# One transformer block on one core: another beginning (order of loads, constants and first stages, and extra identity products on TensorE)

## The chip, the cores and the metric

The kernel runs on one core of a Trainium2 chip. A core has five engines that each run their own list of instructions in order and meet through semaphores: TensorE (PE; its weight loads are shown as PEld), VectorE (DVE), ScalarE (ACT), GpSimd (POOL) and SyncE (SP), which in this kernel only issues DMAs. The metric is the device time of one execution in microseconds. The kernel before took 459.29 us (median of 5 executions, 456.32 to 459.85).

## The reference, cut to what matters

Eight batches of 256 tokens of width 256 pass through an adaptive layer norm, an attention with a window of 64, a second adaptive layer norm and a mixture of 16 experts. Everything that this change touches lies before the first attention scores.

```python
mod = (_silu(L0_c) @ L0_wmod).reshape(8, 6, 1, -1)          # scales, shifts and gates of each batch
sa, ca, ga, sb, cb, gb = (mod[:, i] for i in range(6))       # ga, gb: sign kept, magnitude at least 0.25
h = _layernorm(x) * (1 + ca) + sa
q, k, v = h @ Wq.T, h @ Wk.T, h @ Wv.T                       # rotary embedding on q and k,
q = _layernorm_unit(rope(q)) * 256; k = _layernorm_unit(rope(k)); v = _layernorm_unit(v)
probs = softmax(30 * tanh((q @ k.T / sqrt(32) + mask) / 30))
x = x + ga * ((probs @ v) @ Wo.T)
h = _layernorm(x) * (1 + cb) + sb
x = x + gb * (experts(h, top 4 of 16) + shared(h))
```

## The kernel before, in words

All data is float32. A batch b is a tile `x_b` of 128 partitions by 2 by 256. The first part of the kernel (up to about 185 us) does attention, second norm and routing for the eight batches, software-pipelined: while the scores of batch b are computed, the qkv projection of batch b+2 and the norm of batch b+3 run. Then the tokens, scattered to rows in DRAM by expert, are fetched tile by tile and go through the experts; at the end sums are read back and the result is written.

In the first part the order on PE, DVE and ACT is written out by hand: `when(stage, batch)` emits the instructions of a stage, and each of these three engines runs what was emitted in exactly that order. POOL and SP are ordered by a scheduler; on POOL the helper `in_turn` (L387) forces the named operations into the order in which they were emitted.

The stages of the beginning, with the lines at which they show in the profile:

- Loads (SP, L106 to L144), in this order: c, a third of wmod (`load_mod(0)`, L116), x of batch 0 (L124), wqkv (L126), rope, x of batches 1 and 2, and so on. SP later issues the zero fills `rows_d<-none` and `sums<-none` (L285), the gates `gates_d<-g` (L455), the shared experts' weights, and the row of gates of each batch (`gate<-gates_d`, L474).
- Constants on POOL (L147 to L280): the identity `ident`, `nhalf`, masks, one-hot patterns, counters, and `none`, from which the zero fills are written.
- `condition_stage`: transposes c on PE (L412) and computes silu on DVE and ACT into `scT` (L414 to L420).
- `columns_stage(0)`: 16 products of wmod with `scT` on PE (L429), copied by DVE into `modT` (L433, L434).
- `fold_stage`: two DVE operations that take the mean out of the v columns of wqkv (L461, L462); they wait for wqkv.
- `stats_stage(b)`: the mean and variance of x_b on DVE (L468, L469), then `power` on POOL: an addition (L397) and a power of -0.5 (L398) give `rs`.
- `norm_stage(b)`: `nmr` on DVE (L482), then the normed x on ACT (L487, one instruction for each half).
- `turn_norm_stage(b)`: four PE transposes `pt_a` (L365), then ACT applies `modT` and gives `hT` (L374, two instructions).
- `qkv_stage(b, t)`: two PE matmuls, shown as four passes of 128x384 (L515), then rotary embedding on DVE (L526, L531, L537) and a copy of v on ACT (L536).
- `centre_stage(b)`: two DVE operations over q and k (L545, L546), then squares on ACT (L551, L552).
- `unit_stage(b)`: DVE sums the squares into `rstd` (L560), POOL raises 24 columns of it to the power -0.5 (L397, L398).
- `heads_stage(b)`: DVE multiplies q and k by `rstd` (`qn` L571, `kn` L580), POOL does v (L586); `turn_stage(b)` transposes them on PE (`pt_q`, `pt_k`).
- `rows_stage`: gates on PE (L442), five DVE operations (L449 to L454), the DMA to `gates_d`.

A PSUM tile of the helper `misc` comes from a pool of two buffers; `pt_a`, `pq`, the products of wmod and those of c share them.

Of the kernel before, what the change touches and what calls it, by code (L numbers as in the profile page):

```python
# [9 lines left out]
F32 = mybir.dt.float32  # L10
# [4 lines left out]
ALU = mybir.AluOpType  # L15
# [17 lines left out]
E, INTER, NSH = 16, 176, 2  # L33
TOPK, G, TOPK_G = 4, 4, 2
# [4 lines left out]
CAP = NTOK  # L39
# [5 lines left out]
Q0 = P + SW  # L45
LIVE = P + Q0
HIDDEN = -16.0

ROW = HID + 2 * E
# [9 lines left out]
NOWHERE = float(1 << 20)  # L59
# [8 lines left out]
MAXL = MAXT - MAXA  # L68
# [10 lines left out]
def kernel(  # L79
# [18 lines left out]
    nc = tc.nc  # L98

    const = ctx.enter_context(tc.tile_pool(name="const", bufs=1))  # L100
# [10 lines left out]
    def load_mod(n):  # L111
        nc.sync.dma_start(
            out=wmod_sb[:, :, n * 512 : (n + 1) * 512], in_=wmod_v[:, :, n * 512 : (n + 1) * 512]
        )

    load_mod(0)  # L116
    xs = []
    for b in range(B):
        xs.append(keep.tile([P, NT, HID], F32, tag="x", name=f"x_{b}"))
# [1 line left out]
    def load_x(b):  # L121
        nc.sync.dma_start(out=xs[b], in_=x_in[b].rearrange("(t p) d -> p t d", p=P))

    load_x(0)  # L124
    wqkv_sb = const.tile([P, NK, NH * D], F32)
    nc.sync.dma_start(out=wqkv_sb, in_=wqkvT.rearrange("(k p) n -> p k n", p=P))  # L126
    rope_sb = const.tile([P, NT, 2, D], F32)
# [10 lines left out]
        out=bias_sb,  # L138
        in_=expert_bias.rearrange("(o e) -> o e", o=1).to_broadcast([P, E]),
# [16 lines left out]
    nc.gpsimd.memset(maskb, 0.0)  # L156
    for lo, n in ((0, P), (P, Q0)):
        nc.gpsimd.affine_select(
            out=maskb[:, lo : lo + n], in_=maskb[:, lo : lo + n], compare_op=ALU.is_ge, fill=HIDDEN,
            base=0, pattern=[[1, n]], channel_multiplier=-1,  # L160
        )
        nc.gpsimd.affine_select(
            out=maskb[:, lo : lo + n], in_=maskb[:, lo : lo + n], compare_op=ALU.is_ge, fill=HIDDEN,
            base=SW - 1, pattern=[[-1, n]], channel_multiplier=1,
        )

    pmask = const.tile([P, P], F32)
    nc.gpsimd.memset(pmask, -1.0)
# [1 line left out]


    probs = [const.tile([P, REP, P + S], F32, name=f"probs_{i}") for i in range(KV)]
    for pr in probs:
        nc.gpsimd.tensor_copy(
            pr[:, :, LIVE : P + S], pmask[:, 0 : S - Q0].unsqueeze(1).to_broadcast([P, REP, S - Q0])
        )

    lowG = const.tile([P, G, G], F32)
    nc.gpsimd.memset(lowG, 1.0)
    nc.gpsimd.affine_select(  # L180
        out=lowG, in_=lowG, compare_op=ALU.is_gt, fill=0.0,
        base=0, pattern=[[1, G], [-1, G]], channel_multiplier=0,
    )

    before = const.tile([P, P], F32)
    nc.gpsimd.memset(before, 1.0)
    nc.gpsimd.affine_select(
        out=before, in_=before, compare_op=ALU.is_gt, fill=0.0,
        base=0, pattern=[[1, P]], channel_multiplier=-1,
    )  # L190
    ones = const.tile([P, P], F32)
    nc.gpsimd.memset(ones, 1.0)


    SUMS = KV * NT
    onehot = const.tile([P, SUMS, D], F32)
    nc.gpsimd.memset(onehot, 0.0)
    spread = const.tile([P, SUMS, P], F32)
    nc.gpsimd.memset(spread, 0.0)
    for m in range(SUMS):  # L200
        nc.gpsimd.memset(
            onehot[:, m, :].rearrange("p (a i) -> p a i", i=SUMS)[:, :, m : m + 1], 1.0
        )
        nc.gpsimd.affine_select(
            out=spread[:, m, :].rearrange("p (j d) -> p j d", d=D),
            in_=spread[:, m, :].rearrange("p (j d) -> p j d", d=D),
            compare_op=ALU.not_equal, fill=1.0, base=-m, pattern=[[-D, REP], [0, D]],
            channel_multiplier=1,
        )

    st = const.tile([P, B, NT, 6], F32)
    mv = const.tile([P, B, NT, 2], F32)
    rs = const.tile([P, B, NT], F32)
# [4 lines left out]
    def apart(ins, group):  # L218
# [10 lines left out]
    nc.vector.memset(acc, 0.0)  # L229

    first = const.tile([P, E], F32)
    nc.gpsimd.iota(
        first, pattern=[[CAP, E]], base=1, channel_multiplier=0,
        allow_small_or_imprecise_dtypes=True,
    )

    tno = const.tile([E, MAXL], F32)
    nc.gpsimd.iota(
        tno, pattern=[[1, MAXL]], base=0, channel_multiplier=0,
        allow_small_or_imprecise_dtypes=True,  # L240
    )
    eno = const.tile([P, E], F32)
    nc.gpsimd.iota(
        eno, pattern=[[1, E]], base=0, channel_multiplier=0,
        allow_small_or_imprecise_dtypes=True,
    )
    start = const.tile([E, 1], F32)
    nc.gpsimd.iota(
        start, pattern=[[0, 1]], base=-E * CAP, channel_multiplier=CAP,
        allow_small_or_imprecise_dtypes=True,  # L250
    )
    upto = const.tile([E, E], F32)
    nc.gpsimd.memset(upto, 1.0)
    nc.gpsimd.affine_select(
        out=upto, in_=upto, compare_op=ALU.is_ge, fill=0.0,
        base=0, pattern=[[1, E]], channel_multiplier=-1,
    )


    rows_d = tc.dram_tile([E * CAP + P, ROW], F32, name="rows_d")  # L260
    none = const.tile([P, ROW], F32)
    nc.gpsimd.memset(none[:, 0 : HID + E], 0.0)
    nc.gpsimd.memset(none[:, HID + E : ROW], NOWHERE)

    sums = [tc.dram_tile([NTOK + P, HID], F32, name=f"sums_{i}") for i in range(2)]
    spare = const.tile([P, 1], F32)
    nc.gpsimd.iota(
        spare, pattern=[[0, 1]], base=NTOK, channel_multiplier=1,
        allow_small_or_imprecise_dtypes=True,
    )  # L270
    pno = const.tile([P, 1], F32)
    nc.gpsimd.iota(
        pno, pattern=[[0, 1]], base=0, channel_multiplier=1, allow_small_or_imprecise_dtypes=True,
    )

    tokens = const.tile([P, B, NT, ROW - HID - E], F32)
    nc.gpsimd.iota(
        tokens, pattern=[[S, B], [1, NT], [0, ROW - HID - E]], base=0, channel_multiplier=NT,
        allow_small_or_imprecise_dtypes=True,
    )  # L280
# [61 lines left out]
    with ExitStack() as actx:  # L342
# [8 lines left out]
        def misc(name):  # L351
            return small_ps[0].tile([P, 512], F32, tag="mm", name=name)
# [34 lines left out]
        def in_turn(kind, ins):  # L387

            ins = getattr(ins, "ins", ins)
            for other in last:  # L390
                if kind != "put" or other != "put":
                    tc.add_manual_dep(ins, last[other], BEHIND, reason="order of GpSimd")
            last[kind] = ins.name

        def power(out, in_, eps):

            in_turn("own", nc.gpsimd.tensor_scalar(out, in_, eps, None, ALU.add))  # L397
            in_turn("own", nc.gpsimd.tensor_tensor(out, out, nhalf[:, 0 : in_.shape[-1]], ALU.pow))  # L398
# [574 lines left out]
        when(norm_stage, 0)  # L973
        when(stats_stage, 1)
        when(columns_stage, 0)
        when(turn_norm_stage, 0)
        when(stats_stage, 3)
        when(norm_stage, 1)
        when(qkv_stage, 0, 1)
        when(qkv_stage, 0, 0)  # L980
        when(turn_norm_stage, 1)
        when(centre_stage, 0)
# [12 lines left out]
        for b in range(B):  # L995
# [64 lines left out]
            out=gbs, in_=gates_d[1:2].rearrange("a b d -> a (b d)").to_broadcast([P, B * HID])  # L1060
# [285 lines left out]
```

## Time and profile before

| what | us |
|---|---|
| five executions | 458.76, 459.85, 459.29, 459.45, 456.32 |
| the profiled execution | 458.84 |
| its span, from the first to the last instruction | 456.9 |
| PE, DVE, ACT, POOL busy | 404.8, 257.6, 193.3, 236.5 |
| first `nmr` of batch 0 on DVE | 10.40 |
| first `qn` of batch 0 on DVE | 29.01 |

The span is cut into a beginning, in which engines wait for loads and for each other, and a long middle in which PE is busy nine tenths of the time. In the profile's timeline a row has the start in us, the length in us, the engine, the line, the operation, the tiles (output first) and, in brackets, the idle time of the engine before it with what ended it. Rows that follow each other without a gap are merged. A matmul in float32 shows as two passes. The chain of waits has the start, the length and the engine with tile and line.

### The profile page before, as it was taken

Reading aid. Unit: us, or ns where it says so; the run is one execution under the profiler, and the core shown is the slowest. Engines: PE = TensorE matmul, PEld = TensorE weight load, DVE = VectorE, ACT = ScalarE, POOL = GpSimd, SP = SyncE. Lnnn points to the kernel's source line nnn. Section 1 sums busy time; section 2 is a strip of 40 time slices with the busy share of each in tenths; the row PEclk is TensorE's granted clock in tenths of the full one; section 3 lists DMA queues with packets and bytes.
Section 4 is the critical chain, followed back from the end, with each engine's and each line's share of the span. In section 5 each row is a group of like instructions: output and inputs, shape, how many; then the busy total and the mean of one; then the engine's idle time right before and its main releaser. Section 6 shows DMA issues by size and latency. Waiting matters only on the chain.

```text
span 456.9 us, 8848 instructions
## 1 busy us (share of the span) xinstructions
PE 404.8 (89%) x2790; PEld 287.4 (63%) x2790; DVE 257.6 (56%) x937; ACT 193.3 (42%) x445; POOL 236.5 (52%) x232
## 2 busy tenths in 40 slices
PE   3878999998888857978999999999999999999763
PEld 3446777667666655555677657576777777777332
DVE  5677888987874543265764335425444454434087
ACT  2437788676645614225434321213434444343100
POOL 8155652486867641113566527755565656665200
PEclk9989999999999877797999999999999999999897
DMA  8999973012221210403455525555667666666494
GB/s 266 369 355 316 317 191 104 14 66 82 84 70 40 105 66 8 151 13 113 111 131 132 141 65 86 83 75 96 114 109 118 106 121 112 110 110 100 58 362 167
DMA packets 52926, 59.79 MB, mean 131 GB/s; under 512 B 5272, under 2 KB 47888, under 8 KB 52752
## 3 DMA queue, kind: packets, MB, share of 16 engines
q1 hardware_dynamic: 39728, 40.59, 30.1%
q0 software_dynamic: 13152, 18.62, 22.9%
q8 instruction: 24, 0.39, 0.4%
q14 instruction: 22, 0.18, 0.1%
HBM read 31.51 MB, written 27.69 MB: 130 GB/s over the span
## 4 chain that ended last, share of the span: by engine, by line
PE 69%; DVE 10%; DMA 9%; ACT 5%; issue 3%; POOL 2%; another core or an unknown queue 1%; SPq 1%; DVEq 0%; ACTq 0%; POOLq 0%
PE u L1115 16%; PE py L1141 11%; PE us L1172 7%; DMA sums<-yr,to 7%; PE pq L515 4%; PE pv L648 3%; PE pw L700 3%; PE sm L657 3%; PE xt L1083 3%; PE pz L1188 3%; PE ph L1130 3%; PE sc L621 2%; PE pn L679 2%; PE pr L724 2%; PE sc L612 1%
## 5 line engine op out<-in xcount | busy, mean ns | idle before, releaser
L1155 POOL DMA_INDIRECT sums<-yr,to x70 | 109.2, 1560 | 60.6 <-DVE h L1123 19.4
L928 POOL DMA_INDIRECT rows_d<-pay,idx x64 | 63.2, 988 | 79.7 <-ACT xT L1085 18.7
L1115 PE MATMUL u<-w,xT 128*128 x288 | 98.5, 465 | 0.4 <-issue 0.3
L1141 PE MATMUL py<-w_sb,hT 88*128 x280 | 72.0, 379 | 0.0
L1115 PEld LDWEIGHTS u<-w,xT 128*128 128x128 f32 x288 | 49.6, 192 | 17.0 <-issue 1.3
L1085 ACT COPY xT<-xt 128x256 f32<-128x256 f32 x73 | 27.1, 372 | 73.4 <-PE xt L1083 65.4
L1123 DVE TENSOR_TENSOR h<-h,u 128x176 f32<-128x176 f32 x72 | 24.2, 336 | 50.2 <-ACT h L1122 47.2
L1141 PEld LDWEIGHTS py<-w_sb,hT 88*128 88x128 f32 x280 | 47.6, 190 | 3.8
L1172 PE MATMUL us<-h2T,sw_sb 128*128 128x512 f32 (+1 forms) x96 | 46.0, 630 | 2.6 <-PEq L1258 2.6
L1122 ACT ACTIVATE h<-u 128x176 f32<-128x176 f32 x72 | 22.8, 317 | 58.1 <-PE u L1115 52.4
L1148 DVE TENSOR_SCALAR yr<-py,w 128x256 f32<-128x256 f32 x70 | 33.6, 480 | 11.3 <-PE py L1141 9.1
L1172 PEld LDWEIGHTS us<-h2T,sw_sb 128*128 128x128 f32 (+1 forms) x96 | 18.4, 195 | 25.4 <-issue 25.1
L398 POOL TENSOR_TENSOR rstd<-rstd,nhalf 128x24 f32<-128x24 f32 x8 | 33.8, 4221 | 0.7
L1089 DVE SCALAR_TENSOR_TENSOR both<-eno,whose,xr 128x16 f32<-128x16 f32 x73 | 16.8, 231 | 25.6 <-DMA xr<-rows_d 23.9
L515 PE MATMUL pq<-wqkv_sb,hT 128*128 128x384 f32 x64 | 27.4, 559 | 3.4 <-ACT hT L374 2.0
L1130 PEld LDWEIGHTS ph<-ident,h 128*88 128x88 f32 x142 | 17.2, 122 | 21.0 <-issue 12.2
L1083 PE MATMUL xt<-ident,xr 128*128 128x128 f32 x146 | 28.3, 276 | 0.0
L1188 PE MATMUL pz<-sw_sb,hs 128*128 128x256 f32 (+1 forms) x96 | 24.1, 403 | 4.1 <-DVE hs L1179 3.8
L1130 PE MATMUL ph<-ident,h 128*88 128x128 f32 x142 | 27.2, 273 | 0.4 <-DVE h L1123 0.4
L630 ACT ACTIVATE probs<-sc 128x640 f32<-128x640 f32 x32 | 22.3, 695 | 11.3 <-PE pw L700 9.1
L1132 ACT COPY hT<-ph 88x256 f32<-88x256 f32 x71 | 26.1, 367 | 1.6 <-PE ph L1130 1.4
L1083 PEld LDWEIGHTS xt<-ident,xr 128*128 128x128 f32 x146 | 20.4, 144 | 9.2 <-issue 3.1
(223 smaller groups left out, 657.8 us busy)
## 6 DMA issues: line engine op xcount, KB each, us to landing
xr<-rows_d SPq DMA_DIRECT2D x75, 144.0 KB
w<-in_w_dram SPq DMA_DIRECT2D x16, 352.0 KB
sums<-none SPq DMA_DIRECT2D x2, 2176.0 KB
got<-sums SPq DMA_DIRECT2D x16, 256.0 KB
w_sb<-in_w_dram SPq DMA_DIRECT2D x8, 352.0 KB
rows_d<-none SPq DMA_DIRECT2D x1, 2304.0 KB
x<-in_x_dram SPq DMA_DIRECT2D x8, 256.0 KB
out_dram<-got SPq DMA_DIRECT2D x8, 256.0 KB
```

Of the source, the lines that this page charges most:

```text
L398: in_turn("own", nc.gpsimd.tensor_tensor(out, out, nhalf[:, 0 : in_.shape[-1]], ALU.pow))
L515: ins = nc.tensor.matmul(out=pq[:, 0 : NH * D], lhsT=hT[:, k, t * P : (t + 1) * P], rhs=wqkv_sb[:, k, :], start=(k == 0), stop=(k == NK - 1),)
L928: ins = nc.gpsimd.indirect_dma_start(out=rows_d[:, :], out_offset=bass.IndirectOffsetOnAxis(ap=idx[:, t, k : k + 1], axis=0), in_=pay[:, t ...
L1083: nc.tensor.transpose(pt[:, k, :], x[:, k * P : (k + 1) * P], ident)
L1085: nc.scalar.copy(xT, pt)
L1115: ins = nc.tensor.matmul(out=pu, lhsT=xT[:, k, :], rhs=w13[:, k, bass.ds(e, 1), :].rearrange("p o h -> p (o h)"), start=(k == 0), stop=(k ...
L1130: nc.tensor.transpose(ph[:, i, :], h[:, i * HALF : (i + 1) * HALF], ident)
L1141: nc.tensor.matmul(out=py, lhsT=h[:, i, :], rhs=w2_sb[:, i, bass.ds(e, 1), :].rearrange("p o d -> p (o d)"), start=(i == 0), stop=(i == 1),)
L1148: nc.vector.tensor_scalar(y, py, w, None, ALU.mult)
L1155: ins = nc.gpsimd.indirect_dma_start(out=sums[len(added) % 2][:, :], out_offset=bass.IndirectOffsetOnAxis(ap=to[:, 0:1], axis=0), in_=y, i ...
L1172: nc.tensor.matmul(out=pus[a][:n], lhsT=sw13_sb[:, k, a, c : c + n], rhs=h2T[:, k, b0 : b0 + nb, :], start=(k == 0), stop=(k == NK - 1),)
L1188: nc.tensor.matmul(out=pz[:, t, :], lhsT=hids[b, i][:n, t * P : (t + 1) * P], rhs=sw2_sb[:n, i, :], start=(i == 0), stop=(i == len(SHC) - 1),)
```

## The change

Four things are moved or added; no arithmetic of the result is changed.

1. Loads: x of batch 0 is issued ahead of the first third of wmod.
2. Constants: only `ident`, `nhalf` and `pmask` are made at once. All the others are put in a list `fills`, and `fill_stage(0)` and `fill_stage(1)` emit the first and the second half of it, each in turn with the powers on POOL.
3. `warm_stage(n)`: n products of the identity with itself (float32, 128x128x128) into a `misc` tile that nobody reads: three before the transposes of c, five after.
4. The order of the stages.

```diff
-    load_mod(0)
...
     load_x(0)
+    load_mod(0)
...
+    fills = []
+    def fill(name, *args, **kwargs):
+        fills.append((name, args, kwargs))
...
-    nc.gpsimd.tensor_copy(identb, ident)
...
+    fill("tensor_copy",identb, ident)
+    fill("memset",maskb, 0.0)
...
+        def fill_stage(i):
+            n = len(fills) // 2
+            for name, args, kwargs in (fills[:n], fills[n:])[i]:
+                in_turn("own", getattr(nc.gpsimd, name)(*args, **kwargs))
+
+        def warm_stage(n):
+            pw = misc(f"warm_{n}")
+            for _ in range(n):
+                nc.tensor.matmul(out=pw[:, 0:P], lhsT=ident, rhs=ident, start=True, stop=True)
...
+        warm_stage(3)
         when(condition_stage, 0)
+        when(stats_stage, 0)
+        warm_stage(5)
         when(fold_stage, 0)
-        when(stats_stage, 0)
-        when(stats_stage, 2)
         when(norm_stage, 0)
-        when(stats_stage, 1)
+        fill_stage(0)
         when(columns_stage, 0)
+        when(stats_stage, 1)
+        fill_stage(1)
         when(turn_norm_stage, 0)
-        when(stats_stage, 3)
-        when(norm_stage, 1)
-        when(qkv_stage, 0, 1)
         when(qkv_stage, 0, 0)
-        when(turn_norm_stage, 1)
+        when(qkv_stage, 0, 1)
         when(centre_stage, 0)
+        when(norm_stage, 1)
+        when(stats_stage, 2)
+        when(turn_norm_stage, 1)
         when(norm_stage, 2)
         when(qkv_stage, 1, 0)
         when(unit_stage, 0)
+        when(stats_stage, 3)
         when(rows_stage, 0)
         when(columns_stage, 1)
```

In the built program two more things are seen. The first `power` of batch 0 stands on POOL directly behind the identity; that of batch 1 stands in the middle of the fills, behind the fill of `spread`; those of batches 2 and 3 behind all fills. And on SP the order of the zero fills is another: before, rows_d, one of the two `sums`, then `gates_d<-g`, then the other `sums`; after, `sums`, rows_d, `sums`, then `gates_d<-g`. From the first scores on, PE, DVE and ACT run the same lists as before.

More of the change, by code (lines that the diff above doesn't have):

```diff
@@ L150 @@
     nc.gpsimd.memset(nhalf, -0.5)
+    fills = []
+    def fill(name, *args, **kwargs):
+        fills.append((name, args, kwargs))
     identb = const.tile([P, P], BF16)
-    nc.gpsimd.tensor_copy(identb, ident)
     maskb = const.tile([P, LIVE], BF16)
[L156 to L165, printed above, removed]
     pmask = const.tile([P, P], F32)
@@ L172 @@
     probs = [const.tile([P, REP, P + S], F32, name=f"probs_{i}") for i in range(KV)]
[L173 to L176, printed above, removed]
     lowG = const.tile([P, G, G], F32)
[L179 to L183, printed above, removed]
-    before = const.tile([P, P], F32)
[L186 to L190, printed above, removed]
+    before = const.tile([P, P], F32)
     ones = const.tile([P, P], F32)
-    nc.gpsimd.memset(ones, 1.0)
     SUMS = KV * NT
     onehot = const.tile([P, SUMS, D], F32)
-    nc.gpsimd.memset(onehot, 0.0)
     spread = const.tile([P, SUMS, P], F32)
[L199 to L209, printed above, removed]
     st = const.tile([P, B, NT, 6], F32)
@@ L231 @@
     first = const.tile([P, E], F32)
-    nc.gpsimd.iota(
+    tno = const.tile([E, MAXL], F32)
+    eno = const.tile([P, E], F32)
+    start = const.tile([E, 1], F32)
+    upto = const.tile([E, E], F32)
+    rows_d = tc.dram_tile([E * CAP + P, ROW], F32, name="rows_d")
+    none = const.tile([P, ROW], F32)
+    sums = [tc.dram_tile([NTOK + P, HID], F32, name=f"sums_{i}") for i in range(2)]
+    spare = const.tile([P, 1], F32)
+    pno = const.tile([P, 1], F32)
+    tokens = const.tile([P, B, NT, ROW - HID - E], F32)
+    fill("tensor_copy",identb, ident)
+    fill("memset",maskb, 0.0)
+    for lo, n in ((0, P), (P, Q0)):
+        fill("affine_select",
+            out=maskb[:, lo : lo + n], in_=maskb[:, lo : lo + n], compare_op=ALU.is_ge, fill=HIDDEN,
+            base=0, pattern=[[1, n]], channel_multiplier=-1,
+        )
+        fill("affine_select",
+            out=maskb[:, lo : lo + n], in_=maskb[:, lo : lo + n], compare_op=ALU.is_ge, fill=HIDDEN,
+            base=SW - 1, pattern=[[-1, n]], channel_multiplier=1,
+        )
+    for pr in probs:
+        fill("tensor_copy",
+            pr[:, :, LIVE : P + S], pmask[:, 0 : S - Q0].unsqueeze(1).to_broadcast([P, REP, S - Q0])
+        )
+    fill("memset",lowG, 1.0)
+    fill("affine_select",
+        out=lowG, in_=lowG, compare_op=ALU.is_gt, fill=0.0,
+        base=0, pattern=[[1, G], [-1, G]], channel_multiplier=0,
+    )
+    fill("memset",before, 1.0)
+    fill("affine_select",
+        out=before, in_=before, compare_op=ALU.is_gt, fill=0.0,
+        base=0, pattern=[[1, P]], channel_multiplier=-1,
+    )
+    fill("memset",ones, 1.0)
+    fill("memset",onehot, 0.0)
+    fill("memset",spread, 0.0)
+    for m in range(SUMS):
+        fill("memset",
+            onehot[:, m, :].rearrange("p (a i) -> p a i", i=SUMS)[:, :, m : m + 1], 1.0
+        )
+        fill("affine_select",
+            out=spread[:, m, :].rearrange("p (j d) -> p j d", d=D),
+            in_=spread[:, m, :].rearrange("p (j d) -> p j d", d=D),
+            compare_op=ALU.not_equal, fill=1.0, base=-m, pattern=[[-D, REP], [0, D]],
+            channel_multiplier=1,
+        )
+    fill("iota",
         first, pattern=[[CAP, E]], base=1, channel_multiplier=0,
@@ L235 @@
     )
-    tno = const.tile([E, MAXL], F32)
-    nc.gpsimd.iota(
+    fill("iota",
         tno, pattern=[[1, MAXL]], base=0, channel_multiplier=0,
@@ L241 @@
     )
-    eno = const.tile([P, E], F32)
-    nc.gpsimd.iota(
+    fill("iota",
         eno, pattern=[[1, E]], base=0, channel_multiplier=0,
@@ L246 @@
     )
-    start = const.tile([E, 1], F32)
-    nc.gpsimd.iota(
+    fill("iota",
         start, pattern=[[0, 1]], base=-E * CAP, channel_multiplier=CAP,
@@ L251 @@
     )
-    upto = const.tile([E, E], F32)
-    nc.gpsimd.memset(upto, 1.0)
-    nc.gpsimd.affine_select(
+    fill("memset",upto, 1.0)
+    fill("affine_select",
         out=upto, in_=upto, compare_op=ALU.is_ge, fill=0.0,
@@ L257 @@
     )
[L260 to L267, printed above, removed]
+    fill("memset",none[:, 0 : HID + E], 0.0)
+    fill("memset",none[:, HID + E : ROW], NOWHERE)
+    fill("iota",
         spare, pattern=[[0, 1]], base=NTOK, channel_multiplier=1,
@@ L270 @@
     )
-    pno = const.tile([P, 1], F32)
-    nc.gpsimd.iota(
+    fill("iota",
         pno, pattern=[[0, 1]], base=0, channel_multiplier=1, allow_small_or_imprecise_dtypes=True,
     )
-    tokens = const.tile([P, B, NT, ROW - HID - E], F32)
-    nc.gpsimd.iota(
+    fill("iota",
         tokens, pattern=[[S, B], [1, NT], [0, ROW - HID - E]], base=0, channel_multiplier=NT,
@@ L967, in when @@
                 f(b, *args)
+        warm_stage(3)
         when(condition_stage, 0)
+        when(stats_stage, 0)
+        warm_stage(5)
         when(fold_stage, 0)
-        when(stats_stage, 0)
-        when(stats_stage, 2)
-        when(norm_stage, 0)
-        when(stats_stage, 1)
-        when(columns_stage, 0)
-        when(turn_norm_stage, 0)
-        when(stats_stage, 3)
-        when(norm_stage, 1)
-        when(qkv_stage, 0, 1)
-        when(qkv_stage, 0, 0)
+        when(norm_stage, 0)
+        fill_stage(0)
+        when(columns_stage, 0)
+        when(stats_stage, 1)
+        fill_stage(1)
+        when(turn_norm_stage, 0)
+        when(qkv_stage, 0, 0)
+        when(qkv_stage, 0, 1)
+        when(centre_stage, 0)
+        when(norm_stage, 1)
+        when(stats_stage, 2)
         when(turn_norm_stage, 1)
-        when(centre_stage, 0)
         when(norm_stage, 2)
```

## The prediction

> **What bounds the kernel now.** I read the page first: its 40 slices say whether the beginning is one stall or a chain.
>
> ```profile
> span 456.9 us, 8848 instructions
> ...
> PE   3878999998888857978999999999999999999763
> ...
> PEclk9989999999999877797999999999999999999897
> ```
>
> A slice is 11.4 us. PE is nearly full from the third one on, so time won or lost ahead of the first scores moves everything behind it by as much, unless a later wait absorbs it. What the beginning waits for is in the chain of waits of the first 60 us:
>
> ```profile
> 2.24 5.17 DMA wqkv_sb<-in_wqkvT_dram
> ...
> 10.40 0.17 DVE nmr L482
> ...
> 13.30 4.79 PE pq L515 x8
> ...
> 19.88 1.57 PE pq L515 x4
> ...
> 22.96 0.87 DVE rstd L560
> ...
> 24.55 4.44 POOL rstd L398
> ...
> 29.01 0.70 DVE qn L571
> ...
> 31.36 2.72 PE pq L515 x4
> ```
>
> It runs: wqkv lands (7.41), `nmr` of batch 0 (10.40), its projection (to 18.1), the projection of batch 1 (to 21.4), `rstd` of batch 0 (to 23.83), its power on POOL (to 28.99), `qn`. Note that `rstd` of batch 0 comes behind the projection of batch 1: on DVE it is listed after that projection's rotary embedding. Note also one operation with two speeds: four passes of `pq` take 1.57 us at 19.88, and 2.72 at 31.36.
>
> The stage table, cut at the edges at which the granted clock changes (17.22, 30.87, 34.28: 3.41 us apart or multiples of it), explains that. Columns: busy time of PE, PEld, DVE, ACT, POOL, then the clock.
>
> ```profile
> 6.98:10.39 3.41, 1.98 (x10) 1.88 (x9) 2.65 (x10) 0.00 (x0) 1.99 (x5) 1.00 1.07 346
> 10.39:13.80 3.41, 1.87 (x5) 1.18 (x6) 2.46 (x12) 2.21 (x5) 1.99 (x5) 1.00 1.08 363
> 13.80:17.22 3.42, 3.42 (x6) 1.69 (x6) 0.95 (x3) 0.96 (x2) 0.81 (x2) 1.00 1.09 363
> ...
> 27.46:30.87 3.41, 1.02 (x7) 0.79 (x8) 2.43 (x6) 1.49 (x4) 2.42 (x2) 1.00 1.04 356
> 30.87:34.28 3.41, 3.41 (x9) 1.71 (x8) 1.43 (x3) 1.76 (x4) 0.00 (x0) 0.50 1.03 315
> ```
>
> After a window in which PE was busy 1.02 of 3.41 us the clock is 0.50 for the next; that window is full, and the clock is back. Ahead of 17.2 the table shows 1.00 only because no clock was recorded: the `pq` passes from 14.10 on start 0.64 us apart, later ones 0.32. So PE begins at half speed, windows busy 1.98 and 1.87 do not free it, and one busy 3.42 does. Other windows give the threshold for falling: busy 1.31 (201.54) falls, 1.62 (133.27) stays, 1.68 (177.64) and even 2.31 (153.75) fall.
>
> **The change part by part**, in the time of the profiled execution (458.84 us: its span of 456.9 and 1.9 around it; 0.45 below the median).
>
> *Loads.* x_0 and the first third of wmod swap places; the bytes ahead of wqkv stay the same, so wqkv lands at 7.41 as before. x_0 takes a place whose load, twice its size, was there by 5.38, when the products of wmod began: it lands between 2.5 (where c was used) and 5.4. Its statistics stand behind `scT` on DVE, which comes at about 5.
>
> *Identity products.* The three run from 1.7, when `ident` is made (1.41 + 0.29). Nearest rows: the eight passes of `pn` at full clock took 1.16 us (0.145 each), the 16 passes of `modT_ps` at 5.38, at half clock, 3.58 (0.22). Six passes: 0.9 to 1.3 us, I take 1.3 at half clock, so c's transposes start at 3.0 instead of 2.57. From there to `scT` it took 2.76 (2.57 to 5.33), of which one addition (L418) took 1.08 while its neighbours took 0.25, beside memsets on POOL that are now gone: `scT` at 4.9 to 5.8. Then the statistics (8.07 to 9.23: 1.16) and POOL's power (9.23 to 10.40: 1.17): `nmr` could run at 7.2 to 8.1. The fold, ahead of it on DVE, takes 7.51 to 8.15. So the fold ends last and hides all of this, up to 0 to 0.9 us; `nmr` runs at 8.17, **2.23 us earlier**. The five products take 1.5 to 2.2 us behind c's transposes and lie in the wait for `scT` and wmod.
>
> *First projection.* From `nmr` to the first transpose 0.85 (10.40 to 11.25), so 9.02; to the first `pq` 2.05 before (11.25 to 13.30), 1.7 at full clock: 10.7. PE is now busy without a gap from 1.7 to at least 7.6 (the products of wmod from 5.6, 16 passes at 0.12 as at 23.2), longer than a window and a half, so full clock is granted between 5.1 and 8.5. If it lasts, the two projections end at 10.7 + 2.85 (eight passes at 0.32 and 0.3 of first and last) = 13.55, against 18.07. If the short waits on either side of 9 us (windows busy about half, where the rows above fall both ways) bring half clock back, 5.5 us from 11.1: 16.6. I take 13.55, since 17.22 to 20.63 with 2.04 of 3.41 busy stayed at full clock, and keep 16.6 for the range.
>
> *norm of batch 1, moved behind centre of batch 0.* This gives the head start back. Before, `xn` of batch 1 was ready at 14.76, under the projection, and its transposes followed at once (17.91). Now `nmr` stands on DVE behind centre, and `xn` on ACT behind centre's squares. The two rotary embeddings take 1.48 each (16.27 to 17.75) from 12.3, centre 1.7 (19.62 to 21.31): 16.98. The squares and `xn` follow as at 21.31 to 21.98, so `xn` starts at 17.65; 0.65 to the first transpose, 18.3. Here **PE stands still for 4.7 us**, from 13.55 to 18.3, where before it had 1.4. A gap of 4.7 leaves at least one window of 3.41 no more than 31% busy; the rows with 0.30 and 0.38 fell. So half clock follows: transposes and `hT` as at 11.25 to 13.30 (2.05), `pq` of batch 1 at 20.35; to its embedding 2.97 (13.30 to 16.27), 23.3; embedding 1.39 (21.48 to 22.87) and `rstd` 0.96: 25.65. Before: 23.83. **Loss 1.8 us.** At full clock throughout: 23.9, a loss of nothing. With half clock in both projections, centre ends at 19.8 and `rstd` at 28.4: a loss of 4.6, or 2.5 to 3.5 where only part of the first is slow.
>
> The Trainium skill ("TensorE: Matmul & The Clock Gate", the HAM clock gate) has the array at half rate by default, freed by about 3.4 us of activity and gated again when a wait exceeds about 3.4 us. The rows above agree with its window, and it speaks against this change at just that place: 4.7 is beyond its limit. By it alone the shorter waits near 9 us cost nothing and the sum is the loss of 1.8; by the rows it lies between that and 4.6.
>
> *Statistics of batches 2 and 3.* Batch 2's (1.16) now lie in DVE's wait for `pq` of batch 1 (17 to 23.3). Batch 3's lie behind `rstd`: DVE then has 1.16 + 2.4 (gates and `modT`, 23.91 to 26.32) + 1.5 = 5.1 us ahead of `qn`, and POOL's power takes 5.18 (23.83 to 29.01). Nothing, by a cover of 0.1; without it, their 1.16.
>
> *Fills.* 6.2 us of POOL work moved from 1 to 8 us to 7.4 to 16.5, with one power of 1.1 inside. Batch 1's power sits behind the first half: done by 13.5, wanted at 16.9. Cover 3 us; the first uses of the constants (33.9 on) have more. But `none` is ready at 15.8 instead of 6.7, so SP's zero fills start at 15.8 instead of 12.01: the DMA engines idle some 1.7 us, and `gates_d<-g` now queues behind both `sums`. 6.8 MB (2 x 2176 + 2304 + 144 KB) at the 371 GB/s of 11 to 28 us end at 36.2; the shared weights wait for the gates as before (29.35 was such an end), four issues of 0.47, the row of gates at some 41.5 instead of 40.28. DVE wants it for `wob` at 38.9, here 40.5; what follows has slack until `pt_q` at 43.45, here 45. Nothing; beyond 43 it would cost its delay.
>
> *Second fall of the clock.* Before, the wait of 2.76 us ahead of `pt_q` (27.1 to 29.85) was followed by half clock: the `pq` there took 2.72 against 1.29 at 49.60, and 0.2 more in the transposes: 1.6 us. Now PE's list ahead of that wait ends later and the wait is about 2 us; a window can still fall (41% busy, nearest to the row of 0.38), so I count 0.3 to the good, bounds 0 and 1.6.
>
> **Sum:** +1.8 - 0.3 = +1.5 on 458.84; with the 0.45 by which that execution lies below the median: **460.8 us**.
>
> **Rivals.** (a) *Half clock in both projections.* If the windows around 9 us fall, the loss at `rstd` is 2.5 to 4.6; with 3.5 as the middle, 462.5. It decides as soon as the first `pq` passes start 0.64 apart. For it: the fallen windows with 1.68 and 2.31 busy. Against: the one with 2.04 that stayed. (b) *Faster.* Full clock all through (loss 0), no second fall (-1.6), and wqkv earlier because fewer bytes compete (up to -0.6): 457.1 on the same footing, a little less with a good middle. For it: the head start of 4.5 us at the first projection is real. Against: the gap of 4.7 us. (c) *The row of gates comes late.* If the zero fills start later or run at the 315 GB/s of 31 to 34 us, it lands at 44.5 and `qn` of batch 1 waits: some 1.5 more, 462.3. For it: SP's order; against: the slack of 1.5 to 2. (d) *The products do not warm PE*, because the window that counts must be filled with real use: then the first projection is at half clock, and (a) holds.
>
> **How the numbers follow.** A difference below 0.5% (2.3 us) can't be told from none here. Forecast 0.43, (a) and (d) 0.37, (c) 0.05, (b) 0.15. The forecast's own range is 459.3 to 462.0, nearly all within 0.5% of 459.29 (up to 461.6). With (a) up to 463.8 and part of (b) down to 457.8 the range holds some eight in ten. Faster 0.12: most of (b). Slower 0.43: (a), (c) and the upper edge of the forecast. Same 0.45.
>
> **What the profile after would show.** `nmr` of batch 0 near 8.2, behind the fold; the first `pq` near 10.7 with passes 0.32 apart (else (a)); PE idle some 4.7 us ahead of `pt_a` of batch 1, released by ACT `xn`; `pq` of batch 1 with passes 0.64 apart; `rstd` on POOL near 25.7; `wob` waiting for the row of gates without a wait on PE behind it. The prediction is wrong if `rstd` ends before 24, or if its delay is not found again at the end.

## The result, and the profile after

| | kernel before | changed kernel |
|---|---|---|
| median, us | 459.31 (62 runs, 455.79 to 463.93) | 462.77 (36 runs, 457.9 to 467.36) |
| ratio to the kernel before | 1 | 1.0062, 95% interval 1.0043 to 1.008 |
| the profiled execution, us | 458.84 | 457.89 |
| its span, us | 456.9 | 455.9 |
| first `nmr` of batch 0, us | 10.40 | 7.90 |
| first `qn` of batch 0, us | 29.01 | 33.40 |

The ratios in this document compare fast executions with fast ones, so they are not the quotients of the medians (here 1.0075). The changed kernel is slower by 0.6%: 0.0062 x 459.31 = 2.8 us, by the interval 2.0 to 3.7. The profiled execution of the changed kernel is one of its shortest, and shorter than the profiled one of the kernel before. So the time is read from the medians, and the profile is read for the mechanism.

The page of the changed kernel, its 40 slices:

```profile
span 455.9 us, 8878 instructions
...
PE   7588999998898877977999999999999999999754
...
PEclk9979999999997987797999999999999999999987
```

A slice is again 11.4 us. In the first one PE is at 7 instead of 3: the identity products. In the second it is at 5 instead of 8, and the clock in the third, 22.8 to 34.2 us, is at 7 instead of 8. The chain of waits of the first 50 us says what lies there (start, length, engine, tile):

```profile
11.21 5.50 PE pq L533 x8
...
18.25 0.83 DVE mean L563
19.11 0.84 DVE r L564
19.99 0.62 issue
20.61 0.59 ACT xn L505
...
23.30 2.94 PE pq L533 x4
...
27.74 0.86 DVE rstd L578
...
31.84 5.65 DMA gates_d<-g
...
39.54 5.00 DMA gate<-gates_d
44.64 0.69 DVE wob L707
```

The head start is there: the first projection begins at 11.21 (before 13.30). But it takes 5.50 us, and the chain then goes through `centre` (`mean`, `r`), the squares on ACT (hidden in "issue") and `xn` of batch 1, in place of a second projection that follows at once. The timeline of PE shows the gap; in brackets is PE's idle time and what ended it:

```profile
21.25 1.40 PE L371 MATMUL pt_a<-ident,xn 128*128 128x128 f32 x4 [4.54 <-ACT xn L505]
23.30 2.93 PE L533 MATMUL pq<-wqkv_sb,hT 128*128 128x384 f32 x4 [0.66 <-ACT hT L380]
```

And the stage table, cut at the clock's edges (PE, PEld, DVE, ACT, POOL, then the clock; edges ahead of 17.25 are carried back in steps of 3.41 us, since no clock is recorded there):

```profile
3.59:7.01 3.42, 3.34 (x15) 3.08 (x15) 1.97 (x9) 0.22 (x1) 0.83 (x2) 1.00 1.03 336
7.01:10.42 3.41, 3.41 (x17) 3.15 (x16) 1.48 (x8) 1.09 (x2) 3.11 (x12) 1.00 1.11 356
10.42:13.83 3.41, 2.76 (x5) 1.51 (x5) 0.53 (x3) 1.02 (x2) 3.26 (x15) 1.00 1.06 357
13.83:17.25 3.42, 2.87 (x5) 1.01 (x3) 1.96 (x6) 0.21 (x1) 1.60 (x12) 1.00 0.90 294
17.25:20.66 3.41, 0.00 (x0) 0.00 (x0) 3.27 (x9) 1.22 (x4) 0.00 (x0) 1.00 1.03 339
20.66:24.07 3.41, 2.15 (x5) 1.19 (x6) 0.55 (x3) 2.41 (x6) 0.93 (x2) 0.50 1.03 338
24.07:27.49 3.42, 3.42 (x8) 1.15 (x7) 1.20 (x4) 0.79 (x3) 0.00 (x0) 0.50 1.02 319
```

PE is busy in nearly every moment from 3.59 to 10.42, and yet the projection behind it runs at half speed (5.5 us for eight passes). The clock is free only when that projection is over. Then a whole window passes with PE busy 0.00, and the projection of batch 1 runs at 0.50. Two projections at half clock and a gap of 4.54: `rstd` ends at 28.60 instead of 23.83, and the first `qn` starts 4.4 us later.

How that lateness travels, by one operation of each batch, after minus before: `qn` of batch 0 +4.38, batch 1 +4.39, batch 2 +3.08, and +3.08 unchanged to `qn` of batch 4; +4.44 at `qn` of batch 7, behind two windows at half clock from 140.1 us; +3.26 at `wob` of batch 7. Then DVE's next wait for PE in each kernel, before and after:

```profile
165.77 0.14 DVE L771 TENSOR_SCALAR nti_a<-pn_a 16x1 int32<-16x1 f32 x1 [4.52 <-remote]
```

```profile
165.31 0.15 DVE L789 TENSOR_SCALAR nti_a<-pn_a 16x1 int32<-16x1 f32 x1 [0.79 <-PE sm L675]
```

One execution waited 4.52 us there, the other 0.79: 3.73 of difference, which turns +3.26 into -0.47. So without this wait the profiled execution of the changed kernel would be the longer one. Its span is 1.0 us shorter; the other 0.5 us arise behind this point. The wait is not the change's doing: the profiles of the twelve experiments below have it too, between 0.79 and 4.83.

### The profile page after: what moved, and what is told of

It is laid out like the page before. It is cut to its first block, busy times and chain, and to the rows that moved or that the text cites. A ratio compares the mean times of both kernels' runs of the same rounds, so it can differ in the third digit from the quotient of the medians.

```text
span 455.9 us, 8878 instructions
## 1 busy us (share of the span) xinstructions
PE 409.5 (90%) x2806; PEld 292.2 (64%) x2806; DVE 256.7 (56%) x937; ACT 193.6 (42%) x445; POOL 236.4 (52%) x232
## 4 chain that ended last, share of the span: by engine, by line
PE 67%; DMA 12%; DVE 11%; issue 4%; ACT 4%; POOL 1%; SPq 1%; DVEq 0%; ACTq 0%; POOLq 0%
PE u L1137 15%; PE py L1163 10%; DMA sums<-yr,to 8%; PE us L1194 7%; PE pq L533 4%; PE pw L718 3%; PE sm L675 3%; PE pv L666 3%; PE pz L1210 3%; PE xt L1105 3%; PE ph L1152 3%; PE pn L697 2%; PE sc L639 2%; PE pr L742 2%; PE sc L630 1%
## 5 line engine op out<-in xcount | busy, mean ns | idle before, releaser
L1144 ACT ACTIVATE h<-u 128x176 f32<-128x176 f32 x72 | 22.8, 317 | 57.6 <-PE u L1137 50.7
L1194 PE MATMUL us<-h2T,sw_sb 128*128 128x512 f32 (+1 forms) x96 | 44.6, 614 | 2.5 <-PEq L1280 2.5
L1194 PEld LDWEIGHTS us<-h2T,sw_sb 128*128 128x128 f32 (+1 forms) x96 | 17.8, 188 | 24.5 <-issue 24.1
L648 ACT ACTIVATE probs<-sc 128x640 f32<-128x640 f32 x32 | 22.3, 696 | 11.2 <-PE pw L718 9.1
```

The costliest lines, as they stand in the source:

```text
L1194: nc.tensor.matmul(out=pus[a][:n], lhsT=sw13_sb[:, k, a, c : c + n], rhs=h2T[:, k, b0 : b0 + nb, :], start=(k == 0), stop=(k == NK - 1),)
```

## The experiments

Twelve further kernels were run, four on each of three chips, each beside the kernel before on the same chip (medians there: 457.41, 457.29 and 446.04 us). Ratios are to that. The kernel before was profiled on none of these three chips; its markers are those of the profile shown above, and only those up to `qn` of batch 2 are used. "pq" is the duration of the four passes that follow `pt_k` of batch 0, 1.56 at full clock.

| experiment | `nmr` | `qn` 0 | `wob` 0 | pq | `qn` 2 | ratio |
|---|---|---|---|---|---|---|
| kernel before | 10.40 | 29.01 | 40.28 | 2.93 | 55.40 | 1 |
| changed kernel | 7.90 | 33.40 | 44.64 | 1.56 | +3.08 | 1.0062 (1.0043 to 1.008) |
| e1_norm_early | 7.79 | 29.38 | 42.20 | 2.64 | +0.64 | 1.0011 (0.9965 to 1.0057) |
| e2_none_first | 7.73 | 32.36 | 42.28 | 1.56 | +1.82 | 1.0159 (1.0103 to 1.0216) |
| e3_both | 8.80 | 28.83 | 40.58 | 1.56 | -0.99 | 0.9988 (0.9947 to 1.0028) |
| e4_no_warm | 7.64 | 33.09 | 43.54 | 2.93 | +4.16 | 1.0093 (1.0048 to 1.0138) |
| b1_norm_late | 10.43 | 35.67 | 44.10 | 1.56 | +5.12 | 1.0115 (1.004 to 1.0191) |
| b3_x_first | 9.21 | 27.90 | 39.81 | 2.77 | -1.19 | 1.0003 (0.9959 to 1.0047) |
| e5_stats_early | 8.78 | 27.50 | 40.82 | 2.93 | -0.93 | 0.996 (0.992 to 1.0) |
| e6_gate_early | 7.84 | 27.37 | 38.05 | 1.56 | -3.16 | 0.9968 (0.9934 to 1.0003) |
| f1_after_gate | 7.77 | 33.44 | 43.45 | 2.93 | +4.54 | 1.0069 (1.0036 to 1.0102) |
| f2_no_products | 7.74 | 26.68 | 37.35 | 2.66 | -2.58 | 0.9954 (0.9923 to 0.9984) |
| f3_wide | 7.60 | 28.83 | 38.75 | 2.53 | -0.24 | 0.9939 (0.9907 to 0.9972) |
| f4_x_gate | 9.14 | 27.55 | 38.13 | 2.69 | -1.68 | 0.9938 (0.9909 to 0.9967) |

### First four: parts of the change undone

**e1_norm_early**: the norm of batch 1 is listed ahead of the first projection again, and its transposes directly behind it.

```diff
         when(turn_norm_stage, 0)
+        when(norm_stage, 1)
         when(qkv_stage, 0, 0)
         when(qkv_stage, 0, 1)
+        when(turn_norm_stage, 1)
         when(centre_stage, 0)
-        when(norm_stage, 1)
         when(stats_stage, 2)
-        when(turn_norm_stage, 1)
```

> The changed kernel with one stage put back: the norm of batch 1 is emitted ahead of the first projection again and its transposes directly behind it; everything else as changed. Theory N (the norm behind centre costs the time: TensorE idle 4.5 us, half clock, rstd of batch 0 at 28.6): TensorE has no wait over 1.5 us between 11 and 27 us, rstd of batch 0 ends at 22 to 24, qn of batch 0 at 27 to 29, and the time is 457 to 459, 0 to 0.5% below before. In the built program the gates' write now stands ahead of the second zero fill of sums, so the row of gates should also come by 41 and theory G (that row sets the time) expects the same here; it is the next kernel that parts the two. Rival W (the first projection at half clock, with the products, costs the time): rstd improves by under 1.5 us and 461 to 463 stays.

**e2_none_first**: the two fills of `none` are made at once, ahead of all other fills, so that SP's zero fills can start as before.

```diff
     none = const.tile([P, ROW], F32)
+    nc.gpsimd.memset(none[:, 0 : HID + E], 0.0)
+    nc.gpsimd.memset(none[:, HID + E : ROW], NOWHERE)
...
-    fill("memset",none[:, 0 : HID + E], 0.0)
-    fill("memset",none[:, HID + E : ROW], NOWHERE)
```

> The changed kernel with the fill of none done at once, beside the identity; the order of stages as changed. SP: rows_d, rows_d, sums, sums, gates, so the zero fills start at 12 instead of 14.9. Theory N: rstd ends at 28.6 and qn of batch 0 stands at 33.4 as in the changed kernel, so 461.5 to 463 stays, within 0.3% of it. Theory G (the row of gates, awaited until 44.6 on VectorE, sets the time): wob waits until 41 to 42 only, and 459 to 460.5.

**e3_both**: both of these edits.

> The changed kernel with both: norm of batch 1 early, none at once. SP has before's order again (rows_d, sums, gates, sums). N and G together: qn of batch 0 at 27 to 28, wob at 39 to 40, 456.5 to 458.5: 0.2 to 0.6% below before. Rival W: 460 to 462, because the first projection is still at half clock.

**e4_no_warm**: the changed kernel without identity products.

```diff
-        warm_stage(3)
         when(condition_stage, 0)
         when(stats_stage, 0)
-        warm_stage(5)
```

> The changed kernel without the eight identity products. If they free no clock (in the profile of the changed kernel the first projection's passes start 0.64 us apart although TensorE was busy 0.98 and 1.00 of two windows before): the same time as the changed kernel within 0.3%, 461.5 to 463.5, first pq at 10.7 to 11.2 with passes 0.64 apart. If they help in most executions and the profiled one was unlucky: slower than the changed kernel by 1 us or more. If they cost (they put c's chain 0.6 us later): products of wmod start at 5.4 to 5.7 instead of 6.06 and the first pq 0.4 earlier, 0.4 us or less in all.

Where the norm of batch 1 went back, most of the delay of `qn` of batch 0 went with it: it fell from 33.40 to 29.38 (e1) and 28.83 (e3). Where it stayed behind centre, `qn` came at 32.36 (e2) and 33.09 (e4), and both ratios lie above 1. In time the clean pair is e2 and e3, on one chip and apart by the norm alone: 1.0159 and 0.9988, with intervals that do not meet. e1 does not show it in time by itself: the median of its twelve executions is 460.42 us, above the 457.41 of the kernel before, and one of them took 688.92.

Both e1 and e3 missed their expectations on the slow side: in e1 `rstd` ended at 24.70 (22 to 24 expected) and PE waited 1.69 us once (at most 1.5), `qn` came at 29.38 (27 to 29), in e3 at 28.83 (27 to 28), and neither was faster than the kernel before by the 0.2% or more that e3 was to show.

The products earn nothing that can be measured: without them the ratio is 1.0093, with them 1.0062. The two ran on different chips and the intervals overlap, so a gain of 1 us or so is not excluded.

The time of e2 is a miss that its profile doesn't explain: 1.0159 from six runs, though its markers are better than the changed kernel's. The profiled execution was the shortest of the six (455.94 us; the others took 460.46 to 466.66), so its markers may not stand for the rest.

e1 and e3 also show where a head start of 1.6 to 2.6 us at `nmr` goes. In e3, on DVE:

```profile
21.70 0.16 DVE L500 SCALAR_TENSOR_TENSOR nmr<-mv,rs 128x2 f32<-128x2 f32 x1 [1.14 <-POOL rs L416]
23.16 0.95 DVE L578 TENSOR_REDUCE rstd<-sq 128x24 f32<-128x768 f32 x1
```

The first row is `nmr` of batch 2. Its statistics are listed behind centre here, so DVE waits 1.14 us for POOL's power of them, while the embedding of batch 1, ready on PE, is listed behind that `nmr`, and `rstd` behind the embedding.

### Second four: parts of the change alone, and better orders

**b1_norm_late**: the kernel before, with only the norm of batch 1 moved.

```diff
         when(stats_stage, 3)
-        when(norm_stage, 1)
         when(qkv_stage, 0, 1)
         when(qkv_stage, 0, 0)
-        when(turn_norm_stage, 1)
         when(centre_stage, 0)
+        when(norm_stage, 1)
+        when(turn_norm_stage, 1)
```

> The kernel before, with one edit: the norm of batch 1 (nmr, xn, transposes) is listed behind centre of batch 0 instead of ahead of the first projection. Loads, constants and statistics stay as in the kernel before. Theory N (this placement is the loss): nmr of batch 0 at 10.4 and the first projection ends at 18.1 as before, centre follows, PE stands still some 4.5 us ahead of pt_a of batch 1, half clock in its projection, rstd of batch 0 ends at 29 to 30 (before 23.8), the first qn at about 34, ratio 1.006 to 1.010. Rival G (the late zero fills and the row of gates are the loss, the place of the norm is not): ratio 0.998 to 1.002 here. Rival F (fills between the powers on POOL are the loss): 0.998 to 1.002 too.

This is the clearest of the runs. One edit makes the kernel before slower by 1.15% (six executions, interval 0.4% to 1.9%; 0.6% to 1.0% was expected), and `qn` of batch 0 comes 6.66 us later, where the whole change, with its head start, has 4.38. PE's timeline has the same gap and releaser as the changed kernel:

```profile
13.34 4.68 PE L515 MATMUL pq<-wqkv_sb,hT 128*128 128x384 f32 x8 [0.66 <-ACT hT L374]
22.57 1.39 PE L365 MATMUL pt_a<-ident,xn 128*128 128x128 f32 x4 [4.55 <-ACT xn L487]
```

Rivals G and F, which put the loss on the late zero fills or on the fills between the powers, wanted 0.998 to 1.002. There are no fills between the powers here, and the zero fills start at 11.67, as early as before (12.01). The order on SP did shift as in the changed kernel, both `sums` ahead of `gates_d<-g`, because the gates come later; but `wob` starts at 44.10 without any wait for the row of gates, so that row is not what holds it.

**b3_x_first**: the kernel before, with the two loads exchanged and the statistics of batch 0 ahead of the fold.

```diff
-    load_mod(0)
...
     load_x(0)
+    load_mod(0)
...
+        when(stats_stage, 0)
         when(fold_stage, 0)
-        when(stats_stage, 0)
-        when(stats_stage, 2)
         when(norm_stage, 0)
         when(stats_stage, 1)
+        when(stats_stage, 2)
```

> The kernel before, with x of batch 0 loaded ahead of the first third of wmod and the statistics of batch 0 listed ahead of the fold: the good part of the change alone, constants and all other stages as in the kernel before. If the head start is real without identity products and without late fills: nmr of batch 0 at 8.0 to 8.3 (before 10.40), rstd at 21.6 to 22 (before 23.83), qn at 26.8 to 27; wob then waits for the row of gates, which lands at about 40.3 as before, so that 0 to 2 us are kept: ratio 0.995 to 0.999. If POOL's constants hold back the power of batch 0 (they stand ahead of it on POOL here), nmr comes at 9.5 to 10.4 and the ratio is 0.999 to 1.001.

`nmr` came at 9.21, between the two expectations: on POOL the power of batch 0 stood behind the constants and began at 8.13. So the change's other half, constants behind the first power, was worth 1.3 us of the head start (9.21 against 7.90). `rstd` was 1.1 us ahead of the kernel before, `qn` too; the ratio is 1.0003.

**e5_stats_early**: e3_both with the statistics of batches 2 and 3 ahead of the first projection.

```diff
         when(norm_stage, 1)
+        when(stats_stage, 2)
+        when(stats_stage, 3)
         when(qkv_stage, 0, 0)
...
         when(centre_stage, 0)
-        when(stats_stage, 2)
         when(norm_stage, 2)
...
         when(unit_stage, 0)
-        when(stats_stage, 3)
```

> The third experiment (e3_both) with the statistics of batches 2 and 3 moved ahead of the first projection, so that nmr of batch 2 no longer waits for POOL. Theory S (statistics behind centre cost 1.1 us of DVE time ahead of rstd): rstd ends near 22 instead of 24.1 and qn comes at 26.8 to 27.5 instead of 28.8. Theory C (the row of gates caps the gain): wob stays at 40.3 to 40.8 and the time equals that of e3_both, ratio 0.997 to 1.000. If wob moves with qn, C is wrong: ratio 0.993 to 0.996.

`rstd` ended at 22.3 instead of 24.1 and `qn` came at 27.50, as theory S has it; the gain at `rstd` was 1.8 us, more than its 1.1. `wob` stayed where theory C has it, though the ratio, 0.996, lies between its range and the one that was to speak against it, and e3 ran on another chip:

```profile
40.82 0.71 DVE L707 TENSOR_TENSOR wob<-wo_sb,gate 128x512 f32<-128x512 f32 x1 [3.42 <-DMA gate<-gates_d]
```

**e6_gate_early**: e5, and the row of gates of batch 0 is loaded as soon as the gates are written.

```diff
-            if c == 0:
+            if c == 0 and b not in gas:
                 gas[b] = gate(0, b)
...
         when(rows_stage, 0)
+        gas[0] = gate(0, 0)
```

> e5_stats_early, and the row of gates of batch 0 is loaded directly behind the write of gates_d on SP, ahead of the loads of the shared experts' weights, instead of behind them. Theory C (the row caps the gain): wob at 37 to 38.5 instead of 40.5, everything behind it some 2 us earlier, ratio 0.991 to 0.995. Rival: the row is late because of the bytes of the zero fills that are queued ahead of it, not because of its place among the issues: then it lands at 40 to 41 as before and the ratio equals that of e5_stats_early.

`wob` came at 38.05, as theory C has it, and `qn` of batch 2 lies 3.16 ahead instead of 0.93. But the time is that of e5 (454.86 and 455.0 us), so the ratio missed its expectation. The column pq tells why the profiles promise more than the time: 1.56 here, 2.93 in e5. By the steps from `qn` 0 to `qn` 2 compared further below, about 1.5 of the 2.2 us come from the clock that this one execution happened to have, and are no merit of the edit. `wob` still waited 2.15 us; the profile names a load of the shared weights (`sw_sb`), which `wob` does not read, so what held it then stays open.

### Last four: the row of gates, the products, and a short version

**f1_after_gate**: the changed kernel with the edit of e6_gate_early alone.

> The changed kernel, with one edit: the row of gates of batch 0 is loaded directly behind the write of gates_d, ahead of the loads of the shared experts' weights. In the changed kernel wob of batch 0 waited 2.72 us for that row (until 44.64). Theory C (in the changed kernel, too, the row is on the path): wob at about 42, its wait gone or under 0.5, everything behind it 1 to 2.5 us earlier than in the changed kernel, ratio to the kernel before 1.001 to 1.004. Rival: the late qn of batch 0 (33.4) sets the end alone, PE's list behind it is as late without the wait: wob moves, but the later markers stay 3.1 us behind the kernel before, ratio 1.005 to 1.008.

The wait of 2.72 us ahead of `wob` was gone (`wob` at 43.45), and the time got no better: the ratio is 1.0069, in the rival's range. The rival is supported, not shown: the interval (from 1.0036) and the other chip leave room for 1 us. The markers can't decide it, for in this execution the clock was against f1: with pq at 2.93 `rstd` of batch 1 came 1.6 us later than in the changed kernel, `qn` of batch 1 waited 1.56 us for POOL's power, and `qn` of batch 2 stands at +4.54 rather than +3.08. Here are the windows ahead of and at those four passes, first of f1, then of the changed kernel:

```profile
31.89:35.30 3.41, 1.50 (x12) 1.20 (x12) 3.22 (x8) 1.30 (x4) 1.81 (x4) 1.00 1.04 350
35.30:38.71 3.41, 3.40 (x8) 1.55 (x7) 1.25 (x2) 1.96 (x4) 0.00 (x0) 0.50 0.46 148
```

```profile
30.90:34.31 3.41, 1.78 (x9) 0.85 (x8) 3.32 (x10) 1.13 (x3) 3.33 (x3) 1.00 1.04 348
34.31:37.73 3.42, 3.24 (x20) 1.96 (x24) 2.60 (x6) 2.03 (x4) 0.73 (x2) 1.00 0.74 242
```

PE had the same list up to there. The windows lie 1 us apart in it, so that one holds 1.50 us of work and is followed by half clock, and the other holds 1.78 and is not.

**f2_no_products**: e6_gate_early without `warm_stage(3)` and `warm_stage(5)`.

> e6_gate_early without the two groups of identity products. If the products earn nothing (in e6_gate_early the first projection ran at half clock with them): pq of batch 0 starts within 0.3 us of 10.95, rstd, qn and wob within 0.6 us of e6_gate_early, ratio equal to it within the intervals, 0.992 to 0.999. If they earn something: half clock lasts into the projection of batch 1, rstd ends 1 us or more later than 22.2, ratio 0.998 to 1.003.

The first projection began at 11.18 and took 4.38 us, `rstd` ended at 21.5 and `qn` came at 26.68; ratio 0.9954. `rstd`, `qn` and `wob` are each 0.7 us ahead of e6, just beyond the 0.6 that was allowed. So the time is no worse than with the products (0.9968, on another chip).

**f3_wide**: e6_gate_early with wide products, and a third group in the wait for `xn`.

```diff
-            for _ in range(n):
-                nc.tensor.matmul(out=pw[:, 0:P], lhsT=ident, rhs=ident, start=True, stop=True)
+            for m in ((4,), (4, 2), (4, 2))[n]:
+                nc.tensor.matmul(
+                    out=pw[:, 0 : m * P].rearrange("p (m q) -> p m q", m=m), lhsT=ident,
+                    rhs=ident.unsqueeze(1).to_broadcast([P, m, P]), start=True, stop=True,
+                )
...
-        warm_stage(3)
+        warm_stage(0)
...
-        warm_stage(5)
+        warm_stage(1)
...
         when(columns_stage, 0)
+        warm_stage(2)
```

> e6_gate_early with the identity products made wide and extended: instead of three and five products of 128 columns one of 512, then one of 512 and one of 256, and a further 512 and 256 behind the products of wmod, in the wait for xn; so PE is busy without a gap from 1.6 us to the first projection, and more of that time streams columns. Theory W (long streams of columns count as activity, products of 128 or 8 columns do not): passes of pq of batch 0 0.32 apart, the projection takes 2.9 instead of 5.5, rstd ends at 19.5 to 20.5, qn at 24.7 to 25.7; wob is held by the row of gates at 37 to 38; ratio 0.990 to 0.996. Rival: no product of constants frees the clock: pq at half clock, and the last group delays the first transposes by 1 to 2.5 us, rstd ends at 23 to 25, ratio 0.997 to 1.003.

Here the products did free the clock, as the prediction wanted it for the change. The PE timelines, e6_gate_early and then f3_wide:

```profile
3.48 2.50 PE L411 MATMUL warm<-ident 128*128 128x128 f32 x10
5.79 3.56 PE L447 MATMUL modT_ps<-scT,wmod_sb 128*128 128x8 f32 x16
...
10.95 5.49 PE L533 MATMUL pq<-wqkv_sb,hT 128*128 128x384 f32 x8 [0.65 <-ACT hT L380]
```

```profile
6.40 1.85 PE L450 MATMUL modT_ps<-scT,wmod_sb 128*128 128x8 f32 x16
8.10 1.54 PE L411 MATMUL warm<-ident 128*128 128x512 f32 x4
...
10.73 2.85 PE L536 MATMUL pq<-wqkv_sb,hT 128*128 128x384 f32 x8 [0.65 <-ACT hT L380]
16.57 1.12 PE L371 MATMUL pt_a<-ident,xn 128*128 128x128 f32 x4 [3.00 <-ACT v L557]
```

The projection took 2.85 instead of 5.49. The 2.6 us were lost again at once: `nmr` of batch 1 waited 3.37 us for POOL, whose power for it stands in the middle of the fills (12.99), and behind it on DVE stood the statistics of batches 2 and 3 and then the embeddings of batch 0. PE stood still for 3.00, until ACT's copy of v of batch 0, which came with the first of these embeddings. The window 12.99 to 16.40 held 0.59 us of its work, and the projection of batch 1 ran at half clock. `rstd` ended at 23.74 and `qn` came at 28.83, where theory W had 19.5 to 20.5 and 24.7 to 25.7. The ratio, 0.9939, lies in theory W's range, but it can't be told from those of f2 and f4, which have no products.

**f4_x_gate**: b3_x_first with the early row of gates.

> b3_x_first (the kernel before, x of batch 0 loaded first and its statistics ahead of the fold) with the row of gates of batch 0 loaded directly behind the write of gates_d. Theory C: qn stays at 27.9, wob comes at 37.5 to 38.5 instead of 39.81, later markers 1.8 to 2.6 us ahead of the kernel before (b3_x_first: 1.19), ratio 0.994 to 0.998. Rival: the row lands no earlier, since the bytes of the second sums are queued ahead of it: wob at 39.5 to 40, ratio as b3_x_first, 0.998 to 1.002.

`qn` 27.55, `wob` 38.13, ratio 0.9938: theory C's numbers, but for `qn` of batch 2 (1.68 ahead, where 1.8 to 2.6 were expected) and a ratio just below its range. What the early row of gates adds to b3_x_first (1.0003) is not shown in time: the two ran on different chips. With the load of x, the statistics ahead of the fold and the row of gates, and without products or delayed constants, it is the smallest edit of those that beat the kernel before. The changed kernel was not run on this chip, but f1_after_gate was, with 449.58 us against 443.59. f2_no_products (443.42) and f3_wide (443.67) are equally good.

## Why the prediction was right in its time and wrong in a step

The range (457.8 to 463.8) holds 462.77. The forecast itself (460.8, its own range 459.3 to 462.0) does not: what came is the case given 0.37, (a) with (d), priced 462.5. The range held by this rival's price, not by the forecast's own sum. By the ratio the change is 0.62% slower, a little above the bound of 0.5%, with an interval on both sides of it.

*Loads and `nmr`*: right. 8.17 was predicted, 7.90 measured, directly behind the fold; `scT` was there at 4.9, and the addition ahead of it took 0.17 instead of 1.08.

*Identity products and the first projection*: the step that failed is "full clock is granted between 5.1 and 8.5. If it lasts, the two projections end at ... 13.55". They ended at 16.7. The step took any busy PE for work that frees the clock, and the waits behind that work for harmless. The runs say more, in windows carried back as above. First two windows of e2, then one of e6 (PE first):

```profile
1.68:5.09 3.41, 3.41 (x15) 3.16 (x16) 1.12 (x6) 0.93 (x3) 0.19 (x2) 1.00 0.73 251
5.09:8.51 3.42, 2.44 (x21) 2.19 (x19) 2.00 (x10) 0.59 (x2) 2.19 (x7) 1.00 1.04 344
```

```profile
2.83:6.25 3.42, 3.42 (x17) 3.09 (x16) 1.97 (x9) 0.21 (x1) 0.16 (x1) 1.00 1.02 359
```

In e2, e5 and f3 the windows 1.68 to 5.09, 2.17 to 5.58 and 2.75 to 6.16 held identity products and, but for the two short transposes of c, nothing else, and full clock followed: the products of wmod took 1.92, 1.92 and 1.85. In the changed kernel (3.59 to 7.01), e1 (3.20 to 6.61) and e6 (2.83 to 6.25) the window reached into the products of wmod, which write 8 columns each, and half clock stayed (3.56), also where the window counts as busy for 3.42 of 3.42 us, as in e6. And where it was freed early, it did not last: e2's next window, busy 2.44 of 3.42, and e5's, busy 2.19, were followed by 0.50. Only f3 with its third group kept it up to the projection.

The busy time alone does not decide. e3's window 1.53 to 4.94, busy 3.34 with products, was not followed by full clock (its products of wmod took 3.42), while windows with less busy time but passes of `pq` in them were: 2.87 in the changed kernel (13.83 to 17.25 above) and 3.00 in f4 (11.88 to 15.29). What is counted in a window stays open. So the products' effect was left to where the window fell and, without a filled wait behind them, was nil in these runs. Whether f3 differs by the width of its products or only by their reach to 6.40 was not separated.

*norm of batch 1 behind centre*: right in place, releaser and size. PE idle 4.7 predicted, 4.54 measured; half clock in `pq` of batch 1 (2.93); "With half clock in both projections, centre ends at 19.8 and `rstd` at 28.4: a loss of 4.6" stands against 28.60 and 4.77. b1 shows it by one edit. The term was mis-sized in the sum (1.8) only through the step above. How much of the loss is the gap itself and how much the half clock behind it was not separated by a run.

*Statistics*: right for the changed kernel. Those of batch 2 lay under the projection of batch 1, as predicted, and with them a wait of 1.13 us of `nmr` for POOL. Those of batch 3 used up the cover of 0.1: POOL's power ended at 33.24, and `qn` started at 33.40 behind DVE's own list, so they cost 0.2 us at most. The same place costs 1.8 us of `rstd` once the gap is gone (e3 to e5).

*Row of gates*: wrong in size. It landed at 44.5, not 41.5, the figure of (c), and `wob` waited 2.72. The sum does not come out of its own figures (6.8 MB at 371 GB/s take 18.3 us, which from 15.8 gives 34.1, not 36.2), and the rate was lower: 294 to 348 GB/s in the windows from 13.83 to 34.31, and the write of the gates, issued behind the fills, landed at 37.5. The price of nothing was neither refuted nor shown: f1 took the wait away and its time is no better. With an earlier `qn` the markers say that it matters: e3 and e5 waited 3.24 and 3.42, and kept some 0.5 us less of their head start than the others with the same pq. The time does not show it: e6, without that wait for the row, took as long as e5.

*Second fall of the clock*: 0.3 was counted with bounds of 0 and 1.6; the profiled execution gained 1.3 (from +4.38 to +3.08). It looks like a matter of the single execution: with pq at 1.56 the step from `qn` 0 to `qn` 2 was 0.8 to 1.5 us shorter than before in all five profiles, and with 2.53 and more it was within 0.6 of it in all eight others, whatever the edit.

*Fills*: no cost in the changed kernel, as predicted. The other orders show what lay behind their cover of 3 us: where `nmr` of batch 1 is listed ahead of the first projection, it waited for POOL, 1.17 to 2.21 us in e1, e3, e5, e6 and f2 and 3.37 in f3.

## What to carry to other kernels

Before a stage is moved behind another, ask which engine then has nothing to do until the moved stage is through, and read that gap against the clock's window: here 4.5 us of idle PE cost a second time as a projection at half speed. A head start at the front of a pipeline is worth what the next late thing leaves of it, here in turn a power on POOL, a row of gates and the clock. Work that is meant to keep an engine fast is worth little if waits follow it: of the eight profiles with products only f3, whose last group reached up to the first transposes, had its projection at full clock, and in the others the effect was left to where the windows fell.

## What the runs showed of the hardware

- The clock's windows of 3.41 us start elsewhere in each execution (one began at 3.59 us in the changed kernel, at 3.20 in e1, at 2.83 in e6), so one list of instructions meets them differently: the four passes behind `pt_k` took 1.56 us in five of the profiles and 2.53 to 2.93 in the others. No kernel was profiled twice; that the windows' start alone makes some 1.5 us is argued from f1 and the changed kernel, which have one list on PE up to there.
- All profiles have the wait ahead of `nti_a` on DVE that no edit touches: 0.79 us in some executions (the changed kernel, e2, e3, b1), 1.52 to 1.55 in the four of the last chip, and 3.65 to 4.83 in others (the kernel before, e1, e4, e5, e6, b3). What sets it stays open; the profile names another core or an unknown queue in some cases.
- The kernel before took 457.3 and 457.4 us on two of the experiments' chips and 446.0 on the third, so times from different chips are compared by their ratios only.
